# A graph layer's second adjacency pass in one written TensorE order, with 12 blocks by lists, and the score sums moved to layer 1

## The chip, the cores and the metric

The kernel runs on one core of one Trainium2 chip. Its time is device microseconds of one execution; a kernel is run several times and the median is taken. The core has five engines with an instruction stream each: TensorE (PE in the profile, with its weight loads shown apart as PEld), VectorE (DVE), ScalarE (ACT), GpSimd (POOL) and SyncE (SP). SP issues most of the plain DMAs here, ScalarE some, and POOL the indirect ones (gathers).

## The reference, cut to what matters

Two layers over the same adjacency `adj` (3327 x 3327, about 2 nonzeros in a thousand on average, far denser in the first rows and columns, a full diagonal) and features `x` (3327 x 512). Everything is float32.

```python
# layer 0
h = jnp.maximum(_layernorm(x, axis=-1), 0.0)
h1 = jax.nn.relu(adj @ (h @ W1) + b1)          # W1: 512 x 128
x = x + adj @ (h1 @ W2) + b2                    # W2: 128 x 512
# layer 1
h = jnp.maximum(_layernorm(x, axis=-1), 0.0)
type_sum = adj @ h                              # the same for a and b here
attn_a = sigmoid(concatenate([type_sum, h], 1) @ Wa.T + ba)
attn_b = sigmoid(concatenate([type_sum, h], 1) @ Wb.T + bb)
hw = h @ W_sa
s_left, s_right = hw @ a_sa[0, :512], hw @ a_sa[0, 512:]
e = where(adj != 0, exp(-leaky_relu(s_left[:, None] + s_right[None, :], 0.01)), 0.0)
x_a = (e / (sum(e, axis=1, keepdims=True) + 1e-05)) @ hw
x_b = adj @ (h @ W_gcnb) + b_gcnb
x = x + sigmoid(attn_a * x_a + attn_b * x_b)
```

`_layernorm` subtracts the row's mean and divides by the root of its variance plus 1e-5.

## The kernel before

The nodes are padded to 3328, 26 blocks of 128 (NB). The adjacency arrives transposed (adjT), so that 128 source nodes j lie on the partitions and a chunk of 512 target nodes i (256 in one chunk) along the row. `back` (L70 to 80) is the order of the chunks, from the last nodes (2816) to the first (0, 256 wide).

*Pass 1 (L549 to 596).* For each chunk and each of the 26 source blocks SP loads a 128 x 512 tile of adjT, TensorE multiplies it with u = h @ W1 of the block into acc_u (L568), and VectorE takes the largest entry of each group of 32 targets (L572). From these maxima `make_lists` (L433) makes, for each pair of groups of a target block, the list of source rows that are not all zero: row_h (the row) and row_a (the row within the groups of adjT). `rooms` (L44) says how many times 64 such rows a target block has room for, twice (q = 0, 1). A block in OWN (L41) keeps its diagonal part (`extra`) out of the lists: its own 64 x 64 pieces are loaded directly (`load_own`, L196). POOL makes and gathers: `columns` (`gather_adj`) goes through the blocks and fetches, one indirect DMA for each list, 128 columns' entries into `ae`; `gather_behind` (L216) lets such a gather wait for a matmul through `pace`. `make_g` (L338) applies b1 and Relu and stores g = h1.

*Pass 2 (L613 to 859).* This makes adj @ g, the row x1 = x + (adj @ g) @ W2 + b2, and the normalized row h of layer 1. The last LISTED = 2 chunks of 512 targets, blocks 18 to 25, go by lists: rows of g are gathered from memory (`gather_g`, a ring of 24) and `list_sums` (L767) multiplies each 64-row piece of `ae` with them, 64 x 32 by 64 x 128. The others (0, 512, 1024, 1536 and the 256-wide 2048) are dense, 26 matmuls each into acc_g (L825). The rows of a finished chunk are made by the generator `make_h1` (L639): px = sT @ W2 on TensorE (L663), x1 = px + x on VectorE (L666), `ln_relu` (L230: BATCH_NORM_STATS2 and its aggregate on VectorE, a square root on ScalarE at L238, reciprocal and product on VectorE, Relu on ScalarE at L244), the right score on VectorE, the left score too (both L623), the two own logits (`own_logits`, L627: the h halves of the two attention products) and, for a whole chunk, a turn of the left scores on TensorE with copies by ScalarE into `s_left`. ScalarE stores x1; SP stores the row of h (`store_row`, L636) to h_dram. Two sums over block 0's targets (its row of the output needs nearly all sources) run beside it: `add_hubs` (L704, matmuls at L709) with the weights e of `make_e_hub` (L729), exponentials on ScalarE. Where these steps stand in each engine's order is put down by constants: SUMS names the dense matmuls after which a list step comes (L813), the rest by n % 2, n % 3, n % 4 and `last`, with `queued` (L224) adding an "issue after" order. Gathers of `ae` stand behind dense matmuls (gather_behind) where they are not among the constants' steps. The own logits of the blocks in LATE (L39) and OWN are made in layer 1.

*Layer 1 (L861 to 1138).* The blocks go from 25 down to 1, block 0 by the hub sums. For each, `attend` (L917) gathers the rows of h from h_dram into pairs of a ring (hr, and rows, which was pass 2's ring), adds left and right scores, makes the masked exponentials; `sums` (L968, matmuls at L981) adds both aggregates; `turn` (L988) transposes them on TensorE (L995) and copies them out (VectorE, L1010); `weigh` (L1026) multiplies by W_g (p_b, L1035) and W_sa (p_a, L1042); `finish` (L875) applies the logits, the scaling, tanh in place of the sigmoid, and the store. A block's gathers wait (`pace`, LEAD L27) for the sums three or four blocks earlier; `fetch_ae` takes two gathers of `ae` at a time for the blocks that pass 2 had not reached.

The lists can run out of room; an If at the end (L1141 on) would then compute it all densely. It isn't entered with these inputs.

Of the kernel before, what the change touches and what calls it, by code (L numbers as in the profile page):

```python
# [18 lines left out]
P = 128  # L19
CW = 512  # L20
# [8 lines left out]
LISTED = 2  # L29
LN_EPS = 1e-5  # L30
SUM_EPS = 1e-5
# [7 lines left out]
LATE = 10, 11, 16  # L39

OWN = 1, 6, 7, 8, 12, 13, 14, 15, 17, 18  # L41


def list_rooms(n_blocks):  # L44

    rooms = [0, 8, 7, 6, 5, 5] + 6 * [4]
    return (rooms + n_blocks * [3])[:n_blocks]
# [3 lines left out]
def kernel(  # L51
# [29 lines left out]
    made_order = []  # L81
    for k, c in enumerate(dense_chunks):
        for c0, w in (c, *listed_chunks[k : k + 1]):
            made_order += range(c0 // P, (c0 + w) // P)
# [3 lines left out]
    extra = [int(i in OWN) for i in range(NB)]  # L88
# [29 lines left out]
    bab_row = kept([P, 2], "bab_row")  # L118
    w_own = kept([P, 2, D], "w_own")
# [20 lines left out]
    def segments(i):  # L140

        r = rooms[i] + extra[i]
        n = -(-r // SEG)
        cuts = [-(-r * k // n) for k in range(n + 1)]
        return list(zip(cuts, cuts[1:]))
# [50 lines left out]
    def load_own(i):  # L196

        n = segments(i)[0][1]
        for h in range(2):
            rows = slice(i * P + h * HALF, i * P + (h + 1) * HALF)  # L200
            nc.scalar.dma_start(
                ae[i][h * HALF : (h + 1) * HALF, 0 : n + 1 : n, :GW],
                adjT[rows, rows].rearrange("j (q i) -> j q i", i=GW),
            )
# [25 lines left out]
    def ln_relu(dst, src, pool, name, stats_behind=(), root_behind=(), relu_behind=()):  # L230
# [14 lines left out]
        return scaled, made  # L245

# [12 lines left out]
    with (  # L259
# [35 lines left out]
        def load_weights():  # L295
# [3 lines left out]
            nc.scalar.dma_start(w_own, w_self.partition_broadcast(P))  # L299
            nc.scalar.dma_start(bab_row, b_ab.partition_broadcast(P))  # L300
# [73 lines left out]
        def make_constants():  # L374
# [36 lines left out]
            for r in sorted(set(rooms[1:])):  # L411
                i0, n = rooms.index(r), rooms.count(r)
# [9 lines left out]
                )  # L422
            yield
# [9 lines left out]
        def make_lists(nth, most):  # L433
# [10 lines left out]
            for b in range(w // P):  # L444
                if extra[c0 // P + b]:
                    groups = slice(b * NQ, (b + 1) * NQ)
                    own = flag[:, groups, c0 // P + b]
                    nc.vector.tensor_tensor(own, own, apart, ALU.mult)

# [99 lines left out]
        for n, c in enumerate(back):  # L549
# [37 lines left out]
            with tc.issue_after(chunk_end.ins):  # L587
# [4 lines left out]
                for i in OWN:  # L592
                    if n and c0 <= i * P < c0 + w:
# [25 lines left out]
        acc_hub = [bank(psA, f"acc_hub_{k}") for k in range(2)]  # L619

# [6 lines left out]
        def own_logits(i, h, junk):  # L627

            for s in range(2):
                nc.vector.scalar_tensor_tensor(  # L630
                    junk, h[:, :D], 1.0, w_own[:, s, :], op0=ALU.mult, op1=ALU.mult,
                    accum_out=node[i][:, 1 + s : 2 + s],
                )
            nc.vector.tensor_tensor(node[i][:, 1:3], node[i][:, 1:3], bab_row, ALU.add)

# [3 lines left out]
        def make_h1(c, sT, last):  # L639

            c0, w = c
            blocks = list(range(c0 // P, (c0 + w) // P))
            fetch = iter(blocks)

            def load_next():
                for i in fetch:
                    xs[i] = l0w.tile([P, D], F32, tag="x", name=f"xb_{i}", bufs=5)
                    nc.sync.dma_start(xs[i], x[i * P : (i + 1) * P, :])
                    with queued(last_row[1] if last else None):
                        nc.vector.tensor_tensor(xs[i], xs[i], b2_row, ALU.add)  # L650
                    break

            load_next()
            load_next()
            yield
            for b, i in enumerate(blocks):
                load_next()
                x1 = xs.pop(i)
                while place[i] - NR >= len(e_added):
                    next(hubs)  # L660
                with tc.high_priority():
                    px = bank(psB, f"px_{i}")
                    last_row[2] = nc.tensor.matmul(  # L663
                        px, sT[:, b * P : (b + 1) * P], W2_sb, start=True, stop=True
                    )
                    nc.vector.tensor_tensor(x1, px, x1, ALU.add)  # L666
                    nc.scalar.dma_start(x1_dram[i], x1)
                    h = made_row(i)
                    _, last_row[0] = ln_relu(h[:, :D], x1, l0w, f"b{i}")
                    score(i, h[:, :D], 1, h[:, D : D + 1])  # L670
                if c0:
                    rows_made.add(i)
                yield
                last_row[1] = score(i, made_row(i)[:, :D], 0, node[i][:, 0:1])
                unstored.append(i)
                if last or len(unstored) > 3:
                    store_row(unstored.pop(0))
                if not extra[i] and i not in LATE:
                    own_logits(
                        i, made_row(i),  # L680
                        l0w.tile([P, D], BF16, tag="junk", name=f"junk_{i}", bufs=1),
                    )
                yield
            n = w // P
            pl = bank(psB, f"pl_{c0}")
            for b, i in enumerate(blocks):
# [635 lines left out]
```

## Time and profile before

| what | us |
|---|---|
| runs | 837.87, 833.72, 837.99 |
| median | 837.87 |
| the profiled execution, whole | 834.5 |
| its span, first to last instruction | 832.8 |
| busy PE / PEld | 735.6 / 404.5 |
| busy DVE / ACT / POOL | 506.0 / 194.5 / 461.1 |
| DMA moved | 185.08 MB, 222 GB/s |

The page divides the span into 40 slices and gives each engine's busy share in tenths (a 9 is 90% or more), the granted TensorE clock and the DMA share:

```
PE   9999888989899771899999749967999999999995
DVE  7778868898860611798987225523665557553552
ACT  7770000000000110354544002211212222221121
POOL 2201756766657776534456766674657666767500
PEclk 9999989999999875999999969996999999999999
DMA  8788988988878844789994755664667877767510
```

One slice is 20.8 us. PE reads 9 in most; the slices that read 7 or less fall at 270 to 312, 458 to 500 and 541 to 583 us, and in these the granted clock drops as well. Pass 1 is the first eleven slices. Of the costliest groups of instructions, the largest are POOL's 194 gathers of `ae` (202.6 us, 1.04 each), the 364 instructions of acc_u (161.0), the 260 of acc_g (117.1) and VectorE's 182 maxima (112.3). A float32 matmul is two instructions on TensorE, and a group's mean is the time from start to end of pipelined instructions, so that the pace of one is less than its mean.

### The profile page before, as it was taken

The page shows a single profiled execution, that of the slowest core. Times are in us where ns is not written, and L with a number is a line of the kernel's source. Part 1 is how long each engine was busy: PE and PEld are TensorE (multiplying, and loading weights), DVE is VectorE, ACT ScalarE, POOL GpSimd, SP SyncE. Part 2 cuts the span into 40 slices and gives each one's busy share as a digit, 9 for nine tenths or more (in the row PEclk, how much of TensorE's full clock was granted, in tenths as well). Part 3 has the DMA queues.
Part 4 walks back from the last instruction along what each step waited for, and adds up shares of the span by engine and source line. Part 5 has one row for each costly group of instructions (what it writes and reads, how often), then busy time and mean ns, then how long its engine had stood idle before and what let it go on. Part 6 is the DMA issues. An engine that isn't in the chain of part 4 may idle for free.

```text
span 832.8 us, 11907 instructions
## 1 busy us (share of the span) xinstructions
PE 735.6 (88%) x3595; PEld 404.5 (49%) x3595; DVE 506.0 (61%) x1625; ACT 194.5 (23%) x402; POOL 461.1 (55%) x490
## 2 busy tenths in 40 slices
PE   9999888989899771999899749967999999999995
PEld 7774333444543220444355236633656655665554
DVE  7778868898860611798987225523665557553552
ACT  7770000000000110354544002211212222221121
POOL 2201756766657776534456766674657666767500
PEclk9999989999999875999999969996999999999999
DMA  8788988988878844789994755664667877767510
GB/s 271 245 287 259 326 246 242 293 272 246 232 232 284 262 132 134 240 279 312 327 314 135 241 150 145 199 185 115 195 211 244 255 206 233 240 205 234 178 51 29
DMA packets 104889, 185.08 MB, mean 222 GB/s; under 512 B 18401, under 2 KB 35441, under 8 KB 104818
## 3 DMA queue, kind: packets, MB, share of 16 engines
q1 hardware_dynamic: 66544, 113.43, 41.8%
q0 software_dynamic: 23264, 57.64, 24.3%
q10 hardware_dynamic: 15010, 13.18, 4.9%
q8 instruction: 30, 0.49, 0.2%
q14 instruction: 41, 0.34, 0.1%
HBM read 162.29 MB, written 22.26 MB: 222 GB/s over the span
## 4 chain that ended last, share of the span: by engine, by line
PE 72%; DVE 7%; issue 6%; another core or an unknown queue 6%; DMA 5%; ACT 2%; POOL 1%; SPq 1%; DVEq 0%; ACTq 0%; POOLq 0%
PE acc_u L568 17%; PE acc L981 12%; PE p_b L1035 11%; PE p_a L1042 10%; PE acc_g L825 8%; PE pu L333 3%; PE ptt L995 3%; DMA a<-in_adjT_dram 2%; PE acc_hub L709 2%; PE px L663 2%; PE pt L325 1%; DMA xb<-in_x_dram 1%; PE acc_s L784 1%; DMA hr<-h_rows,row_h 1%
## 5 line engine op out<-in xcount | busy, mean ns | idle before, releaser
L166 POOL DMA_INDIRECT ae<-in_adjT_dram,row_a x194 | 202.6, 1044 | 181.8 <-DVE past L519 54.3
L568 PE MATMUL acc_u<-a,rows 128*128 128x512 f32 (+1 forms) x364 | 161.0, 583 | 0.5 <-DMA a<-in_adjT_dram 0.5
L166 POOL DMA_INDIRECT hr<-h_rows,row_h x120 | 122.7, 1022 | 62.5 <-issue 27.4
L825 PE MATMUL acc_g<-a,g 128*128 128x512 f32 (+1 forms) x260 | 117.1, 584 | 7.2 <-DMA a<-in_adjT_dram 6.8
L572 DVE TENSOR_REDUCE most<-a 128x16 f32<-128x512 f32 (+1 forms) x182 | 112.3, 638 | 11.6 <-issue 6.3
L1035 PE MATMUL p_b<-W_g_sb,tyT 128*128 128x257 f32 x416 | 99.3, 391 | 15.8 <-DVE tyT L1010 15.3
L1035 PEld LDWEIGHTS p_b<-W_g_sb,tyT 128*128 128x128 f32 x416 | 77.8, 192 | 46.5 <-DVE tyT L1010 15.6
L166 POOL DMA_INDIRECT rows<-h_rows,row_h x74 | 75.1, 1015 | 44.3 <-PE acc L981 20.9
L568 PEld LDWEIGHTS acc_u<-a,rows 128*128 128x128 f32 x364 | 67.2, 195 | 58.8 <-issue 56.0
L1042 PE MATMUL p_a<-W_sa_sb,tyT 128*128 128x512 f32 (+2 forms) x216 | 94.2, 577 | 0.2
L1010 DVE COPY tyT<-ptt 128x512 f32<-128x512 f32 x51 | 34.8, 685 | 87.0 <-PE p_a L1042 31.7
L825 PEld LDWEIGHTS acc_g<-a,g 128*128 128x128 f32 x260 | 50.0, 200 | 58.5 <-issue 44.9
L981 PE MATMUL acc<-hr,ae 64*64 64x512 f32 x480 | 68.3, 614 | 4.4 <-issue 4.0
L166 POOL DMA_INDIRECT g_row<-g_rows,row_h x48 | 49.0, 1021 | 20.9 <-issue 13.4
L1042 PEld LDWEIGHTS p_a<-W_sa_sb,tyT 128*128 128x128 f32 x216 | 40.7, 189 | 38.8 <-issue 36.9
L884 ACT ACTIVATE f<-f 128x2 f32<-128x2 f32 x26 | 5.3, 203 | 192.4 <-DVE f L883 97.2
L981 PEld LDWEIGHTS acc<-hr,ae 64*64 64x64 f32 x480 | 27.6, 136 | 33.6 <-issue 33.0
L343 ACT ACTIVATE gT<-acc_u,b_col 128x512 f32<-128x512 f32 (+1 forms) x7 | 4.6, 656 | 163.8 <-DMA a<-in_adjT_dram 90.9
L663 PE MATMUL px<-W_sb,sT 128*128 128x512 f32 x52 | 26.7, 650 | 15.4 <-ACT sT L799 12.0
L666 DVE TENSOR_TENSOR xb<-px,xb 128x512 f32<-128x512 f32 x26 | 17.3, 682 | 36.6 <-PE px L663 28.5
L981 PE MATMUL acc<-rows,ae 64*64 64x512 f32 x296 | 37.1, 593 | 2.5 <-issue 2.3
L623 DVE SCALAR_TENSOR_TENSOR junk<-rows,w_rows 128x512 bf16<-128x512 f32 x52 | 35.6, 684 | 3.2 <-ACT rows L244 1.1
(159 smaller groups left out, 945.2 us busy)
## 6 DMA issues: line engine op xcount, KB each, us to landing
a<-in_adjT_dram SPq DMA_DIRECT2D x286, 256.0 KB
h_rows<-rows SPq DMA_DIRECT2D x26, 260.0 KB
x<-in_x_dram SPq DMA_DIRECT2D x26, 256.0 KB
xb<-in_x_dram SPq DMA_DIRECT2D x26, 256.0 KB
x<-xb ACTq DMA_DIRECT2D x26, 256.0 KB
x1b<-x SPq DMA_DIRECT2D x26, 256.0 KB
out_dram<-va SPq DMA_DIRECT2D x25, 256.0 KB
ae<-in_adjT_dram,row_a POOLq DMA_INDIRECT x194
```

What stands on the lines that cost most here:

```text
L166: return nc.gpsimd.indirect_dma_start(out=dst, out_offset=None, in_=table, in_offset=bass.IndirectOffsetOnAxis(ap=rows, axis=0), bounds_ch ...
L333: nc.tensor.matmul(pu[:, :HID], hT[:, k, :], W1_sb[:, k, :], start=(k == 0), stop=(k == KD - 1))
L568: added = nc.tensor.matmul(acc[:, :w], u[j], a[:, :w], start=(j == 0), stop=(j == NB - 1))
L572: nc.vector.tensor_reduce(most[:, : w // GW, j], a[:, :w].rearrange("p (b i) -> p b i", i=GW), axis=AX.X, op=ALU.max, apply_absolute_value ...
L623: return nc.vector.scalar_tensor_tensor(junk, h, 1.0, w_rows[:, s, :], op0=ALU.mult, op1=ALU.mult, accum_out=into)
L663: last_row[2] = nc.tensor.matmul(px, sT[:, b * P : (b + 1) * P], W2_sb, start=True, stop=True)
L825: added = nc.tensor.matmul(acc[:, :w], g[j], a[:, n % per, :], start=(n == 0), stop=(n == NB - 1))
L981: added = nc.tensor.matmul(taken[i]["acc"][h][q * HALF : (q + 1) * HALF, :], both[half_p, q * n + k, :], taken[i][k0][k][half_p, q, :D], s ...
L995: moved = nc.tensor.transpose(pt[:, k * P : (k + 1) * P], ty[h][:, k * P : (k + 1) * P], ident)
L1010: last = nc.vector.tensor_copy(dst, src)
L1035: nc.tensor.matmul(p_b[n][:, :WH], tyT[:, k, 0, :], W_g_sb[:, k, n * WH : (n + 1) * WH], start=(k == 0), stop=(k == KD - 1),)
L1042: last = nc.tensor.matmul(p_a[:, c0:c1], tyT[:, k, 1, :], W_sa_sb[:, k, c0:c1], start=(k == 0), stop=(k == KD - 1),)
```

## The change

- LISTED goes from 2 to 3: blocks 14 to 25, twelve of them, go by lists; the dense chunks are 0, 512, 1024 and 1536, the last 256 wide. MADE gives the order in which the chunks' rows are made.
- Pass 2's order is written out as a string, PLAN: d is a dense matmul, s and t steps of the list sums and their turn, x a row (`make_row` in place of `make_h1`), l a turn of left scores, h a hub matmul, e a hub weight, a one gather of `ae` behind the last gather of g. Each TensorE step is put behind the one before it (`on_pe`). Outside the first four dense matmuls, gathers of `ae` no longer wait for matmuls.
- Blocks 9, 21 and 24 (TOP) get a second direct part, the first 64 sources of block 0, with one list less room; g and h of these 64 rows are loaded as `g_top` and `h_top`. Rooms and segments are adapted, and the constants are made by runs of equal rooms.
- In pass 2 `ln_relu_by_sum` takes the place of `ln_relu`: the sum comes out of the addition of x1, the variance out of a Square with an accumulator on ScalarE, the inverse root out of Ln and Exp; their table is loaded ahead once, and that of Tanh ahead of layer 1.
- Left scores are made in pass 2 for block 0 and blocks 22 to 25 alone. For the other 21 `own_scores` and `turn_score` make them in layer 1, and so are the own logits of all blocks, from a row of h (`load_row`) that SP loads for each block. The own-logit weights are loaded at the start of layer 1.

```diff
-LISTED = 2
+LISTED = 3
+MADE = "dldlldd"
+PLAN = """
+d25 s1 d3 x1 d3 x1 s1 d2 l1 x1 d1 s1 d2 x1 e2 d5 s1 d2 t1 d2 x1 d2 s1 x1 e2 d6 x1 s1 d3 x1 e2
+d4 s1 d2 x1 l1 h1 s1 x1 e2 h1 t1 h1 a1 h1 d1 a1 d1 x1 a1 h1 s1 h1 x1 a1 e2 h2 a1 d2 a1 d1 s1
...
+d2 a1 h2 x1 a1 h2 a1 x1 h1 a1 h2 a1 h2
+"""
-LATE = 10, 11, 16
-OWN = 1, 6, 7, 8, 12, 13, 14, 15, 17, 18
+TOP = 9, 21, 24
+OWN = TOP + (1, 6, 7, 8, 12, 13, 14, 15, 17, 18)
...
-    rooms = [0, 8, 7, 6, 5, 5] + 6 * [4]
-    return (rooms + n_blocks * [3])[:n_blocks]
+    rooms = [0, 8, 7, 6, 5, 5, 4, 4, 4, 3, 4, 4] + n_blocks * [3]
+    rooms[21] = rooms[24] = 2
+    return rooms[:n_blocks]
...
-    extra = [int(i in OWN) for i in range(NB)]
+    extra = [int(i in OWN) + int(i in TOP) for i in range(NB)]
...
+    def ln_relu_by_sum(dst, src, ln):
+        nc.vector.tensor_scalar(ln[:, 1:2], ln[:, 0:1], -1.0 / D, None, op0=ALU.mult)
+        nc.scalar.activation(dst, src, AF.Square, bias=ln[:, 1:2], accum_out=ln[:, 2:3])
+        nc.scalar.activation(ln[:, 3:4], ln[:, 2:3], AF.Ln, bias=eps, scale=1.0 / D)
+        nc.scalar.activation(ln[:, 4:5], ln[:, 3:4], AF.Exp, scale=-0.5)
+        nc.vector.tensor_tensor(ln[:, 0:1], ln[:, 1:2], ln[:, 4:5], ALU.mult)
+        return nc.scalar.activation(dst, src, AF.Relu, bias=ln[:, 0:1], scale=ln[:, 4:5])
...
-                    nc.vector.tensor_tensor(x1, px, x1, ALU.add)
+                nc.vector.scalar_tensor_tensor(
+                    x1, px, 1.0, x1, op0=ALU.mult, op1=ALU.add, accum_out=ln[:, 0:1]
+                )
...
-                    _, last_row[0] = ln_relu(h[:, :D], x1, l0w, f"b{i}")
+                last_row[0] = ln_relu_by_sum(h[:, :D], x1, ln)
...
+            if i in early:
+                last_row[1] = score(i, made_row(i)[:, :D], 0, node[i][:, 0:1])
...
-        QUIET = 6
-        SUMS = {1: (14, 16, 18, 20, 24), 2: (16, 18, 20, 22, 25)}
...
-                elif c and n % 4:
-                    gather_behind(added)
...
+        def gather_rest():
+            with queued(g_last[0]):
+                next(columns, None)
...
+        for what, n in plan:
+            for _ in range(n):
+                does[what]()
...
+        def own_scores(i):
+            if i not in s_left:
+                nc.vector.scalar_tensor_tensor(
+                    junk, h_own[i][:, :D], 1.0, w_left, op0=ALU.mult, op1=ALU.mult,
+                    accum_out=node[i][:, 0:1],
+                )
+            own_logits(i, h_own[i], junk)
...
+        def turn_score(i):
+            if i in s_left:
+                return None
+            pl = bank(psB, f"pl_{i}")
+            turned = nc.tensor.transpose(pl[:, :P], node[i][:, 0:1].to_broadcast([P, P]), ident)
+            s_left[i] = spw.tile([P, 2 * GW], F32, tag="s_left", name=f"s_left_{i}", bufs=3)
+            for h in range(2):
+                half_p = slice(h * HALF, (h + 1) * HALF)
+                nc.scalar.copy(s_left[i][half_p], pl[half_p, h * HALF : (h + 1) * HALF])
+            return turned
...
         for i in range(NB - 2, 1, -1):
             with queued(*held):
+                load_row(i - 1)
                 for seg in segments(i):
                     made = attend(i, seg)
-            if i == NB - 2:
-                own_of(LATE[2], made[0])
+                own_scores(i - 1)
...
+            with queued(added):
+                added = turn_score(i - 1) or added
```

## The prediction

> **What bounds the kernel now.** I read the stretches first (columns: length; busy us and instructions of PE, PEld, DVE, ACT, POOL; granted clock; DMA share; GB/s), cut where the chain of waits changes its engine.
>
> ```profile
> 0.00:237.60 237.60, 217.49 (x1123) 123.52 (x1124) 194.89 (x550) 51.26 (x113) 115.33 (x155) 0.96 0.85 263
> 237.60:262.20 24.60, 22.85 (x81) 9.34 (x79) 6.58 (x20) 0.59 (x1) 17.22 (x17) 0.93 0.88 294
> 262.20:338.50 76.30, 46.82 (x171) 19.70 (x171) 24.53 (x74) 8.86 (x19) 50.03 (x49) 0.73 0.57 180
> 338.50:471.10 132.60, 124.69 (x427) 60.33 (x425) 104.64 (x359) 58.59 (x104) 70.97 (x66) 1.00 0.84 276
> ```
>
> The first adjacency pass ends at 237.6. The second runs to 471.1 (233.5 us), where layer 1's first sums start. Its middle stretch is the weak one: TensorE is busy 46.8 of 76.3 us at a granted clock of 0.73, and no engine is busier than two thirds. The chain of waits names it:
>
> ```profile
> 265.11 9.13 another core or an unknown queue
> ...
> 308.65 8.78 another core or an unknown queue
> ...
> 318.65 13.65 another core or an unknown queue
> ...
> 406.95 2.58 PE acc_g L825 x6
> ...
> 416.39 2.58 PE acc_hub L709 x6
> ...
> 473.05 16.46 another core or an unknown queue
> ```
>
> ScalarE and VectorE stand for 9 to 16 us though the TensorE results that they read are long made. In all these places POOL issues gathers without a pause, one per 1.30 us (1.00 and 0.30 of issue). Its timeline has long unbroken runs at 80.6 to 105.8, 113.9 to 136.9, 240.1 to 271.7, 274.5 to 295.5, 302.4 to 328.1, 455.6 to 486.7 and 538.9 to 569.9, and in the late part of each one something stalls. From 345 to 452, where gathers wait for dense matmuls and come at half that rate, nothing does. That is a coincidence seven times over, not a known mechanism; the sum below uses its price.
>
> **Second pass, TensorE's work.** At full pace a 512-column instruction takes 0.43 (2.58/6, above), a 256-column one 0.22 (8 in 1.73 at 440.27), one of px 0.46 (3.70/8 at 422.46), a list sum 0.039 (22 in 0.85 at 286.44). Before: dense 208 x 0.43 + 52 x 0.22 = 100.9; px 52 x 0.46 = 23.9; hubs 104 x 0.43 = 44.7; list sums 200 x 0.039 = 7.8; turned scores 5.5; turned lists 1.7; together 184.5. So 49 of the 233.5 us is not work. By the same prices the weak stretch holds 35 us of work (51 dense, 96 list, 16 px instructions, 2.2 of turns) and loses 41; the other 8 are scattered, 2.3 of them at the end.
>
> The change takes away one dense chunk: 26 matmuls, 52 instructions, -22.4. Twelve blocks by lists hold 42 groups of eight instructions (rooms plus direct parts) where eight held 25: 136 x 0.039 = +5.3, and four more turns +0.9. Of 26 score transposes 21 go to layer 1: -4.4. New work: 163.9.
>
> **VectorE and ScalarE in the second pass.** Per row go BATCH_NORM_STATS2 0.680, aggregate 0.161, reciprocal 0.154, product 0.152; for 21 rows the left score (0.684 and 0.080 for its accumulator), for 13 the own logits (1.67). An accumulator read (0.08) and two one-column products (0.15 each) come in: 29.8 + 16.0 + 21.7 - 9.9 = 57.6 us less on VectorE, which was busy 135.8 of 233.5. It is no bound, so only its waits count: TensorE idled 2.2 and 2.5 for it at 355.7 and 403.8. ScalarE loses the table loads (8 at L238, 10 at L250, 1 at L850, 1.28 each, 24.4) and gains a squaring pass, which no row shows: between the copy (0.58) and the biased Relu (0.81), I take 0.81, as the same form with a bias; ln and exp at the root's 0.29: 26 x 1.10 = 28.6. It was busy 68 of 233.5 and hides this. The row's own chain is some 0.25 longer (-1.33 on VectorE, +1.58 with two small products); taken as 0, at most 6.5 if every row is waited for. Loads fall by 26 x 256 KB, gathers of g rise by 20 x 64 KB: some 52 MB in place of 57, 257 GB/s over 202 us, where the stretch from 400 to 425 moved 341. At the first pass's 263 it would be 198 us, still no bound.
>
> **Order and gathers.** The written order replaces the paced gathers. After the built order POOL has 68 g gathers and then 43 of adjacency columns that wait for no matmul: 111 x 1.30 = 144 us without a pause, unless a list sum is late in freeing rows. Before there were 48 and some 77 paced ones. Three earlier runs beside a dense stream cost TensorE 7 of 25 us (80.6), 2.5 of 23 (113.9) and 5.1 of 31.6 (240.1): 0.18 per us. The runs at 274 to 328, 455 and 538 cost 36 of 54, 15 of 31 and 15 of 31: 0.5 and more; there nearly each instruction depended on another engine's answer. The new order puts two or more dense matmuls before each such answer is needed, so I take 0.18: 26 us. Ends: 5 (the 240 run alone) and 70 (0.48).
>
> The tail gets barer. The last row's px to layer 1's first sums took 447.0 to 471.1, 24 us, under 24 hub matmuls. Now 16 remain behind the last row, 13.8 us, so some 9 us idle where 2.3 was. Scattered waits: 4. Sum: 163.9 + 26 + 9 + 4 = 203 against 233.5: **-30.5**.
>
> **Layer 1.** The stretch from 490.3 to the end, 342.5 us, holds 320.0 of busy TensorE:
>
> ```profile
> 471.10:490.30 19.20, 3.85 (x33) 1.70 (x33) 2.64 (x8) 2.02 (x4) 12.59 (x13) 0.66 0.48 136
> 490.30:549.90 59.60, 59.60 (x315) 37.66 (x316) 31.94 (x111) 12.97 (x28) 40.48 (x41) 0.97 0.58 173
> 549.90:577.10 27.20, 15.67 (x45) 4.86 (x43) 4.58 (x20) 1.90 (x5) 15.45 (x16) 0.69 0.49 139
> 577.10:742.60 165.50, 164.96 (x960) 100.65 (x963) 94.14 (x331) 39.43 (x87) 108.02 (x106) 1.00 0.73 224
> ```
>
> After 577 TensorE has no idle time to speak of, so what is added to it counts in full: 21 score transposes +4.4; three more groups of sums (110 for 107, 0.114 an instruction by 38 in 4.35 at 727.7) +2.7. At the entrance three blocks' own logits (6 x 0.764 + 3 x 0.153 = 5.0) stand on VectorE ahead of the first turned copy, where one block's 1.67 stood; the sums and turns cover part: +2 (0 to 3.4). VectorE gains 21 x 0.764 + 16 x 1.67 = 43 on 173 of 342.5 us; its copies at L1010 waited 54 us for TensorE (31.7 and 22.3), which covers it: 0, up to 43 without cover. ScalarE's 42 small copies (0.26) hide too. SP carries 16 more h_own loads, and the own-logit weights (512 KB) behind the last row's store: a late load holds the own score, the reciprocal's product behind it, ScalarE's scaling and so the next p_a. The bank ring does the same, four banks a block instead of three; at 543 to 550 the scaling was done 2.7 us before p_a, and 0.77 is put ahead of it: 0. POOL has 188 + 40 gathers for 194 + 22: 12 x 1.30 = 15.6, against 44.6 of waiting for TensorE: +4 (0 to 15.6). Both stalls, at 473 and 554, have the same run lengths and lead as before, so they stay. Sum: **+13**.
>
> In the first pass six more iota runs on POOL (0.75 each) fall in its 54.3 us wait for the first list: 0. Net -17.5 on the span: 815, and 837.9 - 17.5 = **820** on the median (the profiled execution ran 834.5 with a span of 832.8, 3.4 below the median; I keep that distance).
>
> One rule speaks against the move into layer 1. Gathers there were 1.02 on average and 1.49 at worst beside VectorE, so the 53 added products cost POOL by these rows at most 53 x 0.49 = 26 us, which its waits cover. The Trainium skill, "SBUF — State Buffer" (Who interferes with whom), lets a VectorE instruction with two SBUF inputs lock out a GpSimd instruction that reads SBUF; these products have two such inputs, and a gather reads its row list there. By it each of the 53 would hold a gather for its own length, some 36 us, an estimate. No run here shows it yet, and it is no term of the sum.
>
> **Rivals.** (1) The order removes the stalls: loss 5 instead of 26, 799; 784 if layer 1's second stall (15) goes too. For it: 345 to 452, 94% busy. Against: POOL's run grows. Chance 0.20. (2) The freed time goes back: loss about 44, and all is as before, 838. Chance 0.10. (3) Slower: POOL's unbroken run starves ScalarE and VectorE while the written order lets TensorE do nothing else. At 0.48 per us, the price of the runs at 455 and 538, 144 us cost 69: 863. It decides from a loss of 43.5 on, 0.30 per us. For it: the dropped pacing. Against: list sums that free rows late stop POOL. Chance 0.25. That VectorE binds layer 1 lies in it too.
>
> **How the numbers follow.** The forecast, 803 to 833 by losses of 9 to 39, has 0.45. A measurement of this kernel tells 0.5% (4.2 us) from no change: its three runs lie within 4.3. Faster 0.45 + 0.20 = 0.65, same 0.10, slower 0.25. The range, 784 to 855, takes in rival 1 with the lost stall and most of rival 3.
>
> **What will show it.** Right: the second pass ends near 440 (237.6 + 203), dense instructions are 208, table loads three in all, POOL at 1.30 per gather from 240 to about 390, and stalls of some 26 us in that time. Layer 1 over 350 us from first sums. Wrong: under 10 us of waits for an unknown queue in the second pass (rival 1), over 44 (rival 3), or the turned copies (L1010 before) late for TensorE in layer 1.

## The result and the profile after

The changed kernel is slower: 892.42 us (887.09 to 894.54, four runs) beside 837.14 for the kernel before in the same runs, a ratio of 1.066 (95% interval 1.060 to 1.072). The forecast was 820; the range ended at 855. The profiled execution has a span of 892.5 us, 59.7 more than before: 37.1 of them lie ahead of layer 1's first sums (508.2 against 471.1), 22.6 in layer 1 (384.3 against 361.7 us). Medians in this document are over all executions, while ratios leave out those more than 1.5% above the fastest of their kernel (one of 1017.4 us in e3, three of the six of e18).

These are the stretches of the changed kernel, in the columns of the prediction's first view, cut where TensorE changes its pace:

```profile
237.70:251.50 13.80, 9.86 (x39) 3.91 (x37) 9.11 (x27) 1.13 (x1) 10.74 (x11) 0.84 0.73 218
251.50:281.90 30.40, 15.23 (x32) 4.55 (x30) 2.11 (x6) 0.00 (x0) 18.68 (x19) 0.56 0.26 71
281.90:364.00 82.10, 70.15 (x353) 31.05 (x354) 30.01 (x104) 23.75 (x63) 41.97 (x41) 0.94 0.88 291
364.00:429.20 65.20, 30.86 (x103) 11.82 (x101) 10.35 (x34) 7.92 (x20) 47.50 (x46) 0.63 0.30 83
429.20:496.90 67.70, 67.47 (x233) 34.19 (x231) 42.84 (x154) 34.71 (x90) 3.40 (x4) 0.98 0.67 224
496.90:508.20 11.30, 0.04 (x4) 0.04 (x4) 1.75 (x7) 0.66 (x2) 8.80 (x9) 0.63 0.97 335
```

Two stretches are as weak as the middle of the second pass was before: 251 to 282 and 364 to 429. In both POOL never stops, and the DMA engines, at 0.26 and 0.30, are nearly empty as well. (In the kernel before, the slices of its weak middle that read 7 or less run from 270 to 333 us, not only to 312, and the last of them reads 1.) The chain of waits of the same run has these pieces in them (start, length, cause):

```profile
251.48 24.29 issue
...
388.48 2.46 issue
391.31 2.43 issue
...
424.99 1.09 issue
...
512.89 12.29 another core or an unknown queue
...
587.38 11.41 another core or an unknown queue
```

What "issue" looks like is seen in TensorE's timeline (start, length, operation; in brackets the idle time before it):

```profile
377.85 0.42 PE L809 MATMUL acc_s<-g,ae 64*32 64x128 f32 x8
378.85 0.38 PE L809 MATMUL acc_s<-g_row,ae 64*32 64x128 f32 x3 [0.58 <-issue]
380.30 0.31 PE L809 MATMUL acc_s<-g_row,ae 64*32 64x128 f32 x2 [1.07 <-issue]
...
408.58 1.01 PE L680 MATMUL px<-W_sb,sT 128*128 128x512 f32 x1 [2.43 <-issue]
411.38 1.01 PE L680 MATMUL px<-W_sb,sT 128*128 128x512 f32 x1 [1.79 <-issue]
...
427.48 1.92 PE L680 MATMUL px<-W_sb,sT 128*128 128x512 f32 x2 [0.39 <-issue]
```

Up to 378 list sums go eight or more at a time, at 0.04 us each. From then on instructions come one or two at a time, 0.7 to 2.8 us after the ones before, whatever they are, list sum or px; the distances between the starts are multiples of about 0.70 us. In what follows this pace is called the trickle. At 427.5 the pace is back. POOL's gathers are 1.30 us apart from 362.8 to 425.4, 47 of them, and then pause for 66 us: the trickle starts 15 us into that run and ends 2 us after it. The stretch at 251 is the same beside 32 gathers (233.8 to 275.7): eight of columns, which came late out of the first pass, and 24 of g behind them.

### The profile page after: what moved, and what is told of

Read it like the earlier page. It is cut to its first block, busy times and chain, and to the rows that moved or that the text cites. A ratio compares the mean times of both kernels' runs of the same rounds, so it can differ in the third digit from the quotient of the medians.

```text
span 892.5 us, 12120 instructions
## 1 busy us (share of the span) xinstructions
PE 758.6 (85%) x3695; PEld 397.5 (45%) x3695; DVE 489.7 (55%) x1583; ACT 204.0 (23%) x490; POOL 477.1 (53%) x516
## 4 chain that ended last, share of the span: by engine, by line
PE 69%; issue 10%; DVE 6%; another core or an unknown queue 6%; DMA 5%; ACT 2%; SPq 1%; DVEq 0%; ACTq 0%
PE acc_u L590 15%; PE acc L1055 11%; PE p_b L1109 11%; PE p_a L1116 9%; PE acc_g L850 7%; PE acc_hub L733 4%; PE pu L351 3%; PE ptt L1069 2%; PE px L680 2%; DMA a<-in_adjT_dram 2%; PE acc_s L809 1%; DVE most L594 1%; PE pt L343 1%; PE p_list L535 1%
## 5 line engine op out<-in xcount | busy, mean ns | idle before, releaser
L175 POOL DMA_INDIRECT ae<-in_adjT_dram,row_a x188 | 194.1, 1032 | 134.8 <-PE acc_u L590 80.6
L590 PE MATMUL acc_u<-a,rows 128*128 128x512 f32 (+1 forms) x364 | 168.4, 602 | 4.9 <-DMA a<-in_adjT_dram 4.3
L175 POOL DMA_INDIRECT hr<-h_rows,row_h x120 | 128.2, 1068 | 63.3 <-issue 29.0
L1109 PE MATMUL p_b<-W_g_sb,tyT 128*128 128x257 f32 x416 | 103.4, 394 | 18.3 <-DVE tyT L1084 11.6
L850 PE MATMUL acc_g<-a,g 128*128 128x512 f32 (+1 forms) x208 | 99.9, 608 | 15.4 <-issue 9.2
L175 POOL DMA_INDIRECT g_row<-g_rows,row_h x68 | 69.5, 1023 | 54.4 <-PE acc_s L809 29.9
L850 PEld LDWEIGHTS acc_g<-a,g 128*128 128x128 f32 x208 | 41.3, 207 | 63.1 <-issue 50.7
L684 DVE SCALAR_TENSOR_TENSOR xb<-px,xb 128x512 f32<-128x512 f32 x26 | 17.9, 687 | 77.0 <-PE px L680 58.0
L1055 PE MATMUL acc<-rows,ae 64*64 64x512 f32 x272 | 35.2, 622 | 11.4 <-DMA hr<-h_rows,row_h 11.3
L271 DVE SCALAR_TENSOR_TENSOR ae<-ae 128x192 f32<-128x192 f32 (+2 forms) x29 | 11.8, 413 | 51.9 <-ACT ae L270 32.2
L261 ACT ACTIVATE rows<-xb,ln_b 128x512 f32<-128x512 f32 x26 | 18.8, 723 | 91.7 <-DVE ln_b L260 43.1
L907 DVE SCALAR_TENSOR_TENSOR a_hub<-h_own,w_own 128x512 f32<-128x512 f32 x52 | 35.6, 685 | 0.1
```

The source lines that it names most:

```text
L175: return nc.gpsimd.indirect_dma_start(out=dst, out_offset=None, in_=table, in_offset=bass.IndirectOffsetOnAxis(ap=rows, axis=0), bounds_ch ...
L261: nc.scalar.activation(dst, src, AF.Square, bias=ln[:, 1:2], accum_out=ln[:, 2:3])
L590: added = nc.tensor.matmul(acc[:, :w], u[j], a[:, :w], start=(j == 0), stop=(j == NB - 1))
L850: on_pe[0] = nc.tensor.matmul(acc[:, :w], g[j], a[:, n % per, :], start=(n == 0), stop=(n == NB - 1))
L907: nc.vector.scalar_tensor_tensor(junk, h[:, :D], 1.0, w_own[:, s, :], op0=ALU.mult, op1=ALU.mult, accum_out=node[i][:, 1 + s : 2 + s],)
L1055: added = nc.tensor.matmul(taken[i]["acc"][h][q * HALF : (q + 1) * HALF, :], both[half_p, q * n + k, :], taken[i][k0][k][half_p, q, :D], s ...
```

## The experiments

Runs fell on several chips, so each is compared with the kernel before in runs on the same chip. Times of whole kernels are medians. Each of the first three groups asks whether the gather runs are the cause.

**Gathers alone (e1), and kinds of them (e4).** A small kernel without the computation, here its loop in short:

```diff
+for name, n, every, pause, kind in STAGES:
+    for k in range(n):
+        while done < at: work(); done += STEP      # matmul of ident and a constant; copy on ScalarE
+        g = gather(k, kind)                        # waits only at the start and after a pause
```

> This kernel leaves the whole computation out: TensorE runs one independent fp32 matmul of 512 columns after the other, ScalarE small copies, and POOL issues gathers in fourteen stages (8, 12, 16, 24, 48 thin ones of 128 rows x 128 B in a row; 24 with a pause of 1.3, 3 or 6 us after every eighth, with 0.8 us after each one, and with a POOL memset after every eighth; 24 with rows of 2 KB; 24 with 64 rows instead of 128; 24 direct DMAs; 24 thin ones beside 256 KB loads). Theory A, the length of an unbroken run stalls the other engines (onset at 8 to 14 gathers, until some 2 us after the run): 8 lose nothing, 12 at most 2 us of TensorE, 16 up to 5, 24 some 8 to 14, 48 some 30 to 45; the stages with pauses lose under 3. Theory B, the stalls come from what the engines wait for (loads, list sums, dependent steps) and POOL's run only coincides: no stage loses more than 2 us, the one beside loads perhaps.

In the stage of 48 TensorE's and ScalarE's timelines read:

```profile
154.55 45.53 PE L89 MATMUL acc<-moving,ident 128*128 128x512 f32 x105 [0.81 <-issue]
202.29 0.59 PE L89 MATMUL acc<-moving,ident 128*128 128x512 f32 x1 [2.21 <-issue]
...
236.06 4.45 PE L89 MATMUL acc<-moving,ident 128*128 128x512 f32 x10 [0.30 <-issue]
```

```profile
154.56 32.58 ACT L91 COPY small<-small 128x128 f32<-128x128 f32 x99 [1.10 <-ACT small L91]
187.50 0.63 ACT L91 COPY small<-small 128x128 f32<-128x128 f32 x2 [0.36 <-ACT small L91]
...
210.01 0.30 ACT L91 COPY small<-small 128x128 f32<-128x128 f32 x1 [1.10 <-ACT small L91]
...
236.06 69.81 ACT L91 COPY small<-small 128x128 f32<-128x128 f32 x212 [0.46 <-ACT small L91]
```

The run is from 168.3 to 234.7. ScalarE falls to one copy per 0.7 to 1.4 us 19.2 us into it (18.5 in the stages of 16 and 24), TensorE at 34 us; from 222 on POOL's own gathers are up to 2.8 us apart. 1.3 us after the run all three are at full pace. None of these instructions waits for another engine, so theory B falls. TensorE lost less than theory A said in the stage of 24 (1.7 us) and about its least in that of 48 (20.8 us idle; some 29 us beyond the 0.43 us that each instruction takes at full pace): the engines differ in when they are reached. The later stages of e1, with pauses and other kinds of gathers, decide little, since ScalarE's copies had run out by 306 us and 24 gathers hardly reach TensorE; e4 repeats them.

> The computation is left out again. Beside TensorE's row of independent matmuls ScalarE now copies all the time (a 128x512 and a 128x128 copy per matmul), so that both can show a stall in every stage. POOL's stages: 36 thin gathers of 128 rows; 36 of 64 rows; 36 of 16 rows; 36 of 128 rows of 2 KB; 36 direct DMAs; 36 memsets; 40 thin ones in eights with a pause of 1.3 us, then of 2.6 us; 36 in twelves with 2.6 us; 40 in eights with a long POOL memset between; 36 beside 256 KB loads; 40 beside loads in eights with 1.3 us. Theory A1 (what counts is how long POOL issues indirect DMAs without a pause): ScalarE falls to one instruction per 0.7 us some 18.5 us into each stage of 36 gathers, whatever their rows, and not in the stages of eights, the memset breaking the run as well; 10 to 20 us of ScalarE lost per unbroken stage. Theory A2 (what counts is how many descriptors pile up): 64 rows start the trickle at twice the time or never, 16 rows never, and rows of 2 KB or loads beside them sooner. Memsets alone lose nothing by either.

Stages of the second small kernel, in the columns of the first view: 36 thin gathers, 36 of 64 rows, 36 of 16 rows, 36 with rows of 2 KB, 36 memsets, 40 in eights with 1.3 us of pause, 40 in eights with a memset:

```profile
30.60:77.30 46.70, 37.65 (x82) 15.66 (x82) 0.00 (x0) 31.40 (x77) 35.99 (x36) 0.89 0.07 13
107.50:151.90 44.40, 34.91 (x76) 14.30 (x74) 0.00 (x0) 27.13 (x60) 33.74 (x36) 0.89 0.04 7
186.30:228.60 42.30, 31.09 (x67) 12.72 (x65) 0.00 (x0) 26.91 (x60) 31.64 (x36) 0.87 0.02 2
268.40:315.00 46.60, 38.10 (x85) 16.20 (x84) 0.00 (x0) 32.54 (x76) 35.93 (x36) 0.91 0.67 194
406.10:442.30 36.20, 36.20 (x85) 15.96 (x84) 0.00 (x0) 35.72 (x90) 34.19 (x36) 1.00 0.00 0
467.20:524.50 57.30, 57.30 (x135) 25.46 (x134) 0.00 (x0) 56.79 (x147) 39.91 (x40) 1.00 0.06 12
...
680.90:739.40 58.50, 58.50 (x138) 25.94 (x137) 0.00 (x0) 53.27 (x152) 47.13 (x44) 1.00 0.06 12
```

A1 holds: 128 rows, 64, 16 or rows of 2 KB start the trickle alike, 20 to 25 us into the run, and cost ScalarE 16 to 20 us; moved bytes (2 to 194 GB/s) make no difference. A pause of 1.3 us after eight, or a memset in its place, ends it; POOL busy with memsets alone does nothing. TensorE is reached 28 to 37 us into these runs. Here the trickle outlasts the run, by 3 to 4 us with 128 rows, by 5 with 64 and by 7 with 16. Beside 256 KB loads 36 gathers in a row stall TensorE too, and 40 in eights with 1.3 us between do not (58.20 us busy of 58.20). The direct DMAs were all issued in 19 us, too short to tell.

**The unbroken run taken out of the changed kernel (e2), and put into the kernel before (e3).**

```diff
 def gather_rest():
     with queued(g_last[0]):
-        next(columns, None)
+        gather_behind(on_pe[0])
```

> The changed kernel, with each of the 43 column gathers behind the TensorE step that the written order puts ahead of it, instead of all in a row. Theory A (the unbroken run of 47 gathers at 363 to 425 us stalls all): the trickle at 376 to 428 goes, 35 to 50 us less: 842 to 858. Theory B (the written order lets TensorE do nothing else while it waits): within 8 us of 892.

844.59 us, ratio 1.007 (1.003 to 1.011): 48 us less than the changed kernel took (892.42, and 892.92 on the same chip later, e17), from one wait per gather. The stretch that had 30.86 us of TensorE now has it all:

```profile
364.00:429.20 65.20, 65.04 (x290) 34.22 (x290) 41.99 (x144) 30.66 (x81) 38.35 (x37) 1.00 0.80 244
```

```diff
 elif c and n % 4:
-    gather_behind(added)
+    with queued(last_g[0]):
+        last_g[0] = next(columns, None) or last_g[0]
```

> The kernel before, its order on POOL kept, but the 77 column gathers of the second pass wait for no matmul any more. Theory A: the 58 at the end become one run of 75 us, which costs 20 to 45 us: 855 to 885, with the trickle in the second half of the second pass. Theory B: within 8 us of 837.

(The gathers of g, too, are put behind the last one, which keeps POOL's order.) 898.74 us, ratio 1.074 (1.062 to 1.085): more than expected. Its 62 gathers in a row stand at 336.1 to 418.9:

```profile
336.10:418.90 82.80, 35.28 (x70) 14.51 (x70) 26.96 (x86) 10.79 (x20) 64.20 (x62) 0.69 0.41 121
```

So the pacing that the change dropped, not what the written order asks of TensorE, decides.

**Runs broken by pauses (e5, e6).** Every engine's instructions stay, but from the second pass on POOL does twelve memsets of 128x32 after each eighth gather (in short):

```diff
+if in_row[0] == 8:
+    in_row[0] = 0
+    for _ in range(12):
+        with queued(inst): inst = nc.gpsimd.memset(idle, 0.0)
```

> The changed kernel, each engine's order as it was, but from the second pass on POOL does twelve small memsets (some 1.7 us) after every eighth gather; nothing waits for TensorE that did not before. Theory A: all the trickles of the second pass and of layer 1 go (45 us at 376 to 428, 24 at 251 to 276, some 15 at layer 1's entrance, some 15 in its middle), and the pauses give back a part where TensorE waits for gathers: 795, 780 to 820. Theory C (only the wait for TensorE helps, since it holds POOL back to TensorE's pace; 1.7 us in 12 is too little beside the loads): 860 to 892.

> The kernel before with the same pauses. Theory A: the stalls at 265 to 332, 473 to 490 and 554 to 572 go, some 60 us, and the pauses cost up to 15 where TensorE waits for gathers: 790, 775 to 805. Theory C: within 10 us of 838. The distance from the run above to this one is what the change is worth when no gather run is too long: by the sums of the prediction without any such loss some 10 to 20 us less for the changed kernel.

848.22 (1.010, 1.002 to 1.019) and 830.42 (0.989, 0.983 to 0.996): both miss theory A's points, by 53 and 40 us, and the second is within theory C's 10 us of 838. The stretches tell the two apart: the first sums of layer 1 come at 448.9 and 456.7 instead of 508.2 and 471.1, as theory A wants, but layer 1 takes 397.8 and 371.2 us: with the gaps the pause is 2.9 us, and POOL became layer 1's bound.

**Short pauses (e7), and the changed kernel with fewer gathers left for layer 1 (e8).** Four memsets instead of twelve, 1.4 us with the gaps; e8 also has e2's edit and

```diff
 for _ in hubs:
-    pass
+    gather_behind(on_pe[0])
```

> The kernel before with a short pause, four small memsets (some 0.7 us, with the gaps 1.4), after every eighth gather from the second pass on. If a pause of that length breaks a run as well as a longer one, and the longer ones only made POOL the bound of layer 1: first sums of layer 1 at 452 to 460 instead of 471, layer 1 in 345 to 355 us, 800 to 812 in all. If short pauses don't reset what a run uses up: 825 to 838.

> The changed kernel with its column gathers behind TensorE steps, 16 more of them behind the last hub matmuls (24 instead of 40 left for layer 1), and the same short pauses. First sums of layer 1 at 445 to 455, layer 1 in 360 to 370 us: 808 to 825. If what the change moved into layer 1 is no burden once POOL has less to do there: layer 1 under 352 us and at most 805.

793.51 (0.954, 0.942 to 0.965) and 805.99 (0.976, 0.965 to 0.987). Both are well under the 831.96 of the kernel before on that chip (its runs lie between 824.63 and 843.92); the first gained more than expected. The edit of e8 put 10 gathers there and left 30 for layer 1, not 16 and 24 as the expectation says. Layer 1 in e7 and in e8:

```profile
442.70:793.40 350.70, 325.32 (x1798) 191.29 (x1798) 177.56 (x625) 75.61 (x166) 226.18 (x306) 0.98 0.63 187
```

```profile
445.80:801.10 355.30, 332.75 (x1843) 187.89 (x1843) 199.38 (x695) 84.63 (x203) 233.94 (x313) 0.97 0.65 191
```

TensorE has 7.4 us more to do in e8, and layer 1 is 4.6 longer. The second pass of e8 ended at 424.1 on TensorE; the gathers put into its tail held up those of layer 1 until 432, so that 21.7 us went by without a matmul.

**The moved products left out (e9), the old variance (e10).** On top of e8:

```diff
 def own_scores(i):
-    ...
+    nc.vector.memset(node[i][:, 1:3], 0.0)
 def turn_score(i):
-    ...
+    s_left[i] = s_left[NB - 1]
+    return None
```

> The run above, but the left scores (beyond the first five blocks) and the own logits are left out altogether: their products, the 21 transposes and the 42 small copies. Theory L (these lengthen layer 1, by TensorE's transposes and by VectorE work in the way of gathers and of turned copies): 10 to 20 us less than the run above. Theory R (layer 1 is longer because of the gathers left for it and the added groups of sums): within 6 us, some 4.4 for the transposes.

> The run above that, but the second pass normalizes as before: BATCH_NORM_STATS2, the aggregate, the square root on ScalarE with its table loads, reciprocal and product (the sum out of the x1 addition is still made and not used). As predicted (VectorE and ScalarE are no bound in the second pass): within 5 us. Rival (the table loads of 1.28 us stand in each row's chain, and TensorE now waits for rows in its written order): 8 to 25 us more.

e9: 812.78 (0.979, 0.968 to 0.990), layer 1 359.4 us. Leaving the work out gains nothing, so not theory L; theory R's few us are less than these runs can tell. e10: 817.58 (0.984, 0.970 to 0.997), first sums at 456.1 where e9, with the new variance, has 455.6, but e8, whose second pass is e9's, 445.8. The median of e10 is 11.6 us above that of e8, which fits the rival and not the forecast; but the intervals of e8, e9 and e10 overlap, and two executions of one second pass lie 10 us apart. So what the variance costs, nothing or up to some 12 us, is not settled.

**The same short pauses on both kernels, side by side (e11, e12; again e15, e16).** e11 is the changed kernel with the short pauses alone, e12 has e2's edit too.

> The changed kernel and nothing but the short pauses after every eighth gather (the same edit as in the run of the kernel before with short pauses, 793.5 us). Theory A (long runs are the whole difference): second pass and entrance by the prediction's own sums without stalls, first sums of layer 1 at 430 to 442; layer 1, with 40 column gathers left for it, 355 to 370 us; 790 to 812. If the 43 column gathers without a wait still collide with the written order: first sums past 450 and over 820.

> The same with the 43 column gathers behind TensorE steps, that is the run with 16 more gathers in the tail, without these 16. If they held up layer 1's entrance there (first sums at 445.8 after TensorE had done its last hub matmul at 424): first sums at 432 to 438. If the 40 gathers in layer 1 make POOL its bound: layer 1 at 368 to 378 us instead of 355, 802 to 815 in all; if they don't: 788 to 796.

772.53 (1.052, 1.047 to 1.057) and 773.04 (1.053, 1.048 to 1.057): faster than expected and yet slower than before, because here the kernel before takes 734.42 us. In e11's first pass POOL issues 64 gathers without a pause (119.6 to 205.0) and TensorE is busy 82.6 of those 85.4 us:

```profile
119.60:205.00 85.40, 82.62 (x386) 38.71 (x384) 84.57 (x223) 2.75 (x4) 65.88 (x64) 1.00 0.98 308
```

This chip does not have the stalls, so the questions of the two expectations stay open. Both kernels, unedited, were asked for:

> The changed kernel, unedited, where possible on a chip on which the kernel before takes some 734 us. If the long runs' stalls are the whole loss and absent there: 715 to 745 (ratio 0.97 to 1.015), the run of 47 gathers with TensorE at full pace beside it. If the change costs in itself (layer 1's added work and gathers, the barer tail): 746 to 770, ratio 1.02 to 1.05. On a chip with the stalls: 880 to 900 beside 838, as before.

> The kernel before, unedited, for a trace of it on the same chip. Without stalls: 728 to 740, first sums of layer 1 by 425, layer 1 in 310 to 325 us, granted clock 0.98 or more. On a chip with them: as the first trace, 838.

They fell on a chip with stalls: 887.77 beside 836.33 (1.060, 1.056 to 1.065), and 839.13. Then e11 and e7 once more, together:

> The changed kernel with the short pauses, and in the run below the kernel before with the same pauses, on one chip. On a chip with the stalls (before 838): theory A, the long runs are what made the change slower by 55 us: 785 to 810, within 15 us of the run below. Theory L, the work moved into layer 1 costs in itself, whatever the runs: over 20 us more than the run below, layer 1 at 360 us or more against 350. On the chip without stalls: 772, and by the distance to the run below as well.

> On a chip with the stalls: 788 to 805. On the chip without them the pauses can only cost, where POOL is the bound of layer 1 or TensorE waits for a gather: 734 to 755.

770.08 (1.048, 1.043 to 1.052) and 756.28 (1.029, 1.024 to 1.034) beside 734.34, on another chip without stalls. The 13.8 us between them are within theory A's 15, but on a chip where nothing stalls that decides nothing on theory A. From the second pass to layer 1's first sums, and in layer 1, the changed kernel (e15) and the kernel before (e16), both with pauses, read:

```profile
230.00:398.40 168.40, 156.03 (x694) 74.18 (x692) 82.78 (x291) 66.07 (x172) 123.75 (x168) 0.97 0.85 274
398.40:410.70 12.30, 0.05 (x2) 0.01 (x1) 2.32 (x9) 0.72 (x2) 7.95 (x12) 0.64 0.82 285
410.70:590.00 179.30, 177.09 (x978) 100.87 (x978) 113.20 (x397) 45.14 (x111) 135.84 (x180) 0.99 0.69 200
590.00:769.50 179.50, 151.57 (x865) 84.65 (x865) 89.70 (x312) 37.27 (x93) 109.77 (x146) 0.94 0.61 181
```

```profile
230.00:415.00 185.00, 173.45 (x619) 81.02 (x617) 128.40 (x427) 67.52 (x122) 138.95 (x187) 0.97 0.88 288
415.00:418.10 3.10, 0.07 (x3) 0.01 (x2) 1.27 (x5) 0.63 (x2) 2.14 (x3) 1.00 0.50 129
418.10:590.00 171.90, 166.77 (x941) 98.12 (x942) 96.14 (x327) 40.33 (x88) 127.39 (x172) 1.00 0.68 200
590.00:752.40 162.40, 146.16 (x858) 88.82 (x856) 81.45 (x299) 33.68 (x79) 97.49 (x134) 0.95 0.65 191
```

Without stalls the change shortens the second pass by 16.6 us, lengthens the gap ahead of layer 1 by 9.2 and layer 1 by 24.5. That is with pauses in both; the changed kernel unedited on such a chip was tried once more and again fell on one with stalls (e17: 892.92 beside 838.72, 1.063, 1.055 to 1.072).

> The changed kernel, unedited. On a chip without the stalls (before 734): the pauses cost the kernel before 22 us there and the changed one with them takes 770, so without them 745 to 752 if they cost it as much, and 735 to 745 if POOL, with more gathers in layer 1, lost more by them; under 730 (the forecast's direction) only if the pauses cost it 40. On a chip with the stalls: 885 to 895 beside 836.

**Pauses up to the tenth block of layer 1 only, in the kernel before (e18).**

```diff
 for i in range(NB - 2, 1, -1):
+    if i == 15:
+        in_row[0] = None
```

> The kernel before, with the short pauses up to the tenth block of layer 1 and none after, where its gathers come in eights with waits of their own. On a chip with the stalls: 785 to 800, no worse than with pauses throughout (793.5 beside 832). On a chip without: 736 to 746, against 756 with pauses throughout and 734 with none. If it stays above 752 there, the cost lies in the second pass and not in layer 1.

827.17 (0.981, 0.974 to 0.988) on a chip with stalls: a miss. Up to the tenth block of layer 1 its program is that of e7, yet in its profiled execution (833.93 us) layer 1's first sums come at 470.6 instead of 442.7. So pauses of 1.4 us do not help equally everywhere; whether that goes with the chip or changes from execution to execution is not shown. So e7 is the best version on the chip where it ran, and the unedited kernel before is on a chip without stalls, 22 us ahead of it; one version for both was not found.

## Why the prediction was wrong

*Where the time went, in one table (profiled executions).*

| kernel | first sums of layer 1 | layer 1 | span |
|---|---|---|---|
| before | 471.1 | 361.7 | 832.8 |
| after | 508.2 | 384.3 | 892.5 |
| e2, after with paced gathers | 464.6 | 382.0 | 846.6 |
| e3, before without pacing | 536.1 | 357.6 | 893.7 |
| e7, before, short pauses | 442.7 | 350.7 | 793.4 |
| e8, after paced, short pauses, fewer gathers left | 445.8 | 355.3 | 801.1 |
| e15, after, short pauses, chip without stalls | 410.7 | 358.8 | 769.5 |
| e16, before, short pauses, chip without stalls | 418.1 | 334.3 | 752.4 |

*The step that failed: the price of POOL's unbroken run.* The reading that such runs coincide with stalls was right, and e1, e2 and e3 show that they cause them. The step "the new order puts two or more dense matmuls before each such answer is needed, so I take 0.18: 26 us" was wrong: dense matmuls cover nothing, since every instruction is held, dependent or not (e1). Nor is it a rate over the whole run. The two long runs lost 24 us of 41.9 and some 45 of 62.5 (the trickle from 378.3 to 427.5 holds 4.4 us of work at the prediction's prices), 69 together where the sum had 26: each loss is the run's length less some 18 us. The trickle starts 17.7 and 15.5 us into them, about where ScalarE is reached in e1; why TensorE is reached sooner here than in e1 (34 us) no run shows. In e3 the same rule gives 65 us for the run of 82.8, and layer 1's first sums come 65.0 later there.

The mixed price came from runs of 23 to 31 us, of which little lies past that point. That is rival 3, which had 0.25 and the right cause, the unbroken run without pacing, but not the right way: it had the written order keep TensorE from other work, where independent instructions are held as well (e1) and the same order with paced gathers loses nothing in this stretch (e2). That its 0.48 over 144 us gave the same 69 is luck: it counted one run where list sums broke the middle into eights. The 29 us that its 863 still lacks are smaller losses. The term for scattered waits, 4, came to some 26 (270.5 us of second pass less 163.9 of work, the 69 and a tail of 11.3): 12 of them stand at 282 to 364, where eights of g gathers follow each other after 1 to 6 us, and the rest is not traced. Layer 1 adds 10.

*The work of the second pass* was nearly right. The sum gave 20.6 us less (184.5 to 163.9); e15 against e16 show 16.6. *The tail* was right: 9 us were predicted idle behind the last row; it was 11.3 (496.9 to 508.2), and 9.2 more than before in e15 against e16.

*Variance and table loads* were put at no cost; e8, e9 and e10 can't tell that from up to 12 us.

*Layer 1* was mis-sized: +13 predicted, +22.6 measured. Its TensorE part, 7.1, agrees with e7 and e8 (7.4), less with e15 and e16 (15.8, at a granted clock of 0.96 against 0.98). The moved products, taken as hidden, cost nothing that can be seen beside a scatter of 10 us (e9). What was too small is, as far as the runs show, POOL's term, 4 (0 to 15.6): the 40 column gathers left for layer 1 keep POOL behind TensorE, the pauses between its eights disappear, and runs of 16 to 18 form (575 to 597, 599 to 621, 679 to 703), which trickle again. With pauses layer 1 is 29.0 us shorter in the changed kernel (e8) and 11.0 in the kernel before (e7), and e8's is only 4.6 longer than e7's. But e8 also leaves 30 gathers instead of 40, e7 and e8 did not run beside the two unedited traces, and the two edits of e8 were not tried apart on a chip with stalls, so that this part is argued and not shown. On chips without stalls the 24.5 us come with pauses that make POOL dearer still, so that what layer 1 costs there unedited stays open, and with it whether the change is slower there at all.

*The rule weighed against the trace.* The gathers of h took 1.068 and 1.065 us on average (hr, rows) against 1.022 and 1.015 before, and 1.016 and 1.024 in e9, without the products, where e8, with them, has 1.062 and 1.045. So the moved work does stretch them, by 7 to 9 us of POOL's time in all (0.05 x 188 = 9 against before), under the 26 that the rows allowed; e9 also leaves out the transposes and small copies, so that the products are not singled out. The Trainium skill, "SBUF — State Buffer" (Who interferes with whom), is right in direction here; the 36 us estimated by it were four to five times too much.

*The evidence that was there.* The trace of before had runs of eight in layer 1 with 1.8 us between them, and not one of them stalled, while those of 17 and more did. Sorting the runs by their length, instead of dividing loss by length, would have pointed to a threshold and to a price near rival 3's for 47 gathers; but not safely, since two runs of 24 gathers there, at 240 and at 455, lost 5 and 15 us.

## What to carry to other kernels

Gathers issued by POOL in one go can, on some chips, hold up every engine, including ones that have nothing to do with them; so look at POOL's timeline for runs of more than about 14 (18.5 us at 1.30 each) and break them, by a wait that they don't need or by a pause, and keep the pauses where POOL isn't the bound. A wait that looks useless ("pace") may be what keeps a kernel fast: before dropping one, find what it spaces out. When a loss is divided by a length to get a price, check first on the shortest cases whether it is proportional at all.

## What the runs showed of the hardware that was not expected

- Past some 18 to 25 us of indirect DMAs in a row, ScalarE and then TensorE (28 to 37 us in the small kernels, 15 to 18 in the changed kernel), at the end POOL itself, issue one instruction per about 0.70 us or a multiple, independent or not, until 1 to 2 us after the run (3 to 7 in e4). 16 rows or 128, 128 B or 2 KB each: ScalarE is reached after 20 to 25 us in all of them. What is used up in the chip no run here shows. All times here come from executions that the hardware profiler recorded, so that its recording may have a part in the stall is a rival that no run rules out.
- The stall goes with the chip that a run fell on: four had it, one of them each of four times, and two did not. Whether the chip itself makes it or something around it is not shown. The kernel before took 832 to 841 us (medians; one execution taken alone 820) on the chips with it and 734 on two others, with a granted clock of 0.93 to 0.96 and of 0.98 to 1.00; on one of the two 64 gathers in a row cost TensorE under 3 us.
- Where it stalls, DMA engines run empty as well (a share of 0.30 from 364 to 429), so a drop of the transfer rate beside a busy POOL is a sign of it, not a cause.
- The Trainium skill, "SBUF — State Buffer" (Who interferes with whom), says that PE and ACT never wait on anyone, and means SBUF's ports; in e1 both waited, 21 us of idle TensorE in the stage of 48, while the only other activity was POOL's gathers.
